# Group-norm statistics of images 2 to 4 gathered in the first image's steps, with a new table of step offsets

## The chip, the cores and the metric

The kernel runs on one core of a Trainium2 chip. The metric is the device time of one execution in microseconds, the median of several runs. Engines are named as the profile names them: PE (TensorE matmul), PEld (its weight loads), DVE (VectorE), ACT (ScalarE), POOL (GpSimd), SP (SyncE, which issues most DMAs).

## What is computed

```python
# x: (4, 64, 64, 96); a group norm per image, then two layers
x = x + conv(gn(x))                    # layer 0
t = tokens(x)                          # (4, 4096, 96)
t = t + attn(ln(t))                    # linear attention, 6 heads
t = t + ffn(ln(t))                     # 96 -> 384 -> 96, values rounded to fp8 and fp16
...
def gn(v, G=32, eps=1e-5):             # mean and variance of each image and group of 3 channels
    m = mean(g, axis=(1, 2, 4)); s = var(g, axis=(1, 2, 4))
    return (g - m) / sqrt(s + eps)
...
def conv(x):                           # a layer norm, a projection, a scan over the 4096 positions
    A, B, C = proj of xn, each (L, 96, 16)
    h = d * (A * h) + d * (B * u)      # one step of the scan
    y = gate * sum(C * h, over 16 states)
```

The group norm needs all 4096 positions of an image before the image's first chunk can begin.

## The kernel before

An image is cut into 8 chunks of 512 positions, so there are 32 chunks, numbered 0 to 31; image b has chunks 8b to 8b+7. A chunk is worked on in 12 steps (`NT`), one for each pair of a state group `sh` (4) and a channel group `cg` (3). Step k belongs to chunk k // 12; its place in the chunk is called r0 to r11. There are 384 steps (`K`).

The core of a step is a pipeline over tiles of 128 x 512. For tile k: PE makes `b_proj`, `a_proj` and `c_proj`, each of three matmuls (L269, into PSUM banks of the tags B, A, and C or D in turn); ACT copies B to SBUF (`b_copy`, L833); POOL multiplies it with the repeated row (`b_mul`, L836, tile `bu`); DVE multiplies A (`a_mul`, L845), scans (`scan`, L852) and multiplies by C (`c_mul`, L876). For the places in `ON_POOL` the last product is split between ACT (`c_copy`, L882) and POOL (`c_mul_pool`, L885). In step s the program emits `b_proj` and `b_copy` of tile s+3, `a_proj` of s+1, `c_proj` of s, `keep` of s-1 (ACT, L862), `b_mul` of s+2, `c_mul_pool` of s-1, `scan` of s, `a_mul` of s+1, `c_mul` of s; after these the step's other calls in the order in which they were entered (`at`), and last `c_copy`. Every engine keeps its order. PSUM has two A banks, one each of B, C and D, and three of the tag M for everything else.

All other work of a chunk is put into steps by hand. The table `AT` gives each piece an offset; a piece of chunk n runs at step 12n plus its offset. Ahead of the chunk (`front`): `load_x`, `centre` and `scale` (POOL, L692 and L695), `stats` (DVE), `rstd` (POOL), `apply` (ACT, L399), `transpose` (PE), `affine` and `upper` (ACT, L710 and L714), `low` (DVE, L719), then the projections d and u with `d_out` (ACT, L731) and `du_out` (DVE, L735). Their rows go to DRAM (`write`, L769) and come back repeated over 128 partitions (`read`, four DMAs at L776, tile `rep`), which `b_mul` and `a_mul` of the chunk need. Behind the chunk (`tail`): `state_sum` (PE, L900), `gated` (DVE), `project_out` (PE, L943), `residual` (DVE, L948), a layer norm, `transpose_a`, `keep`, `spill`, and the Gram matrix. One image later (`ffn`): `fetch`, `attention`, a layer norm, three pairs of `hidden` and `relu`, `project_f`, `round_out`, `bias_out`, `total`, `store`. `gather` adds the partial products of a chunk by DMA (POOL's queue). What does not fit ahead of step 384 is ordered by a planner (`Plan`) that searches 1500 random orders with estimated costs.

The group norm of image 0 is made in a planned start. That of a later image is made during the image before: for each of its 8 chunks, `load_gx` brings the positions into the tile `gx` (one buffer, 192 KB, SP, L130), `sums` transposes them (PE, four transposes, L546) into an M bank, and `sums_out` one step later has ACT sum them and their squares (L577: two passes, each with a read of the accumulator). `first` makes a further transpose of the first chunk for a shift two steps ahead. After the last sum a chain of eleven small pieces, one per step (DVE, POOL, PE, ACT), ends in the tile `gmr` with mean and factor, which `centre` and `scale` use. The sums' places:

```python
when = [s0 + AT["sums"] + NT * n for n in range(NCH)]
if b == 1:
    when = [8, 15, 22, 29, 36, 43, 50, 57]
...
at(max(when[n] - 7, when[n - 1]), load_gx, b, n)
```

With `sums` at -31 these are steps 65, 77, ..., 149 for image 2 and 161, ..., 245 for image 3.

Of the kernel before, what the change touches and what calls it, by code (L numbers as in the profile page):

```python
# [9 lines left out]
F32 = mybir.dt.float32  # L10
# [7 lines left out]
P = 128  # L18
B, H, W, C = 4, 64, 64, 96
# [3 lines left out]
J = 4  # L23
TC = P * J
NCH = L // TC
# [3 lines left out]
NT = NCG * NSH  # L29
# [8 lines left out]


AT = {  # L40

    "load_x": -39, "centre": -25, "scale": -24, "stats": -22, "rstd": -22, "apply": -21,
    "transpose": -14, "affine": -13, "upper": -13, "low": -12, "proj_d": -9, "d_out": -9,
    "proj_u": -9, "du_out": -9, "write": -9, "read": -6, "proj_gate": -3, "gate_out": -1,

    "gather1": 7, "gather2": 11, "gather3": 14,

    "state_sum": 18, "gated": 18, "project_out": 19, "residual": 19, "stats_a": 20,
    "rstd_a": 21, "apply_a": 22, "transpose_a": 33, "keep": 34, "spill": 39, "gram": 24,
    "gram_out": 24, "gram_add": 26,  # L50

    "fetch": 21, "attention": 26, "residual_f": 26, "stats_f": 26, "rstd_f": 27, "apply_f": 29,
    "transpose_f": 30, "quant_in": 31, "hidden0": 37, "relu0": 37, "hidden1": 31, "relu1": 33,
    "hidden2": 38, "relu2": 38, "project_f": 40, "round_out": 40, "bias_out": 40, "total": 46,
    "store": 51,

    "sums": -31, "sums_out": -30,
}
ON_POOL = (0, 2, 7, 8)
XBUFS = 15  # L60


@with_exitstack
def conv_attn_hybrid_kernel(
# [26 lines left out]
    small = ctx.enter_context(tc.tile_pool(name="small", bufs=4))  # L91
# [4 lines left out]
    BUFS = {  # L96
        "x": XBUFS, "gx": 1, "z": 2, "xat": 1,
        "lo": 1, "xs": 2, "xl": 2, "dd": 1, "rep": 2, "gate": 2,
# [112 lines left out]
    for r in range(2):  # L211
        t = const.tile([P, J, CA], F32, tag=f"xa{r}", name=f"xa{r}")
        nc.gpsimd.memset(t[:, :, C:CA], 1.0)
        xa_t.append(t)
        t = const.tile([CA, J, P], F32, tag=f"xal{r}", name=f"xal{r}")
# [3 lines left out]
        t = const.tile([P, J, P], F8, tag=f"xn8{r}", name=f"xn8{r}")  # L219
# [144 lines left out]
    class LayerNorm:  # L364
# [3 lines left out]
            self.eps, self.nm, self.r = eps, nm, None  # L368

        def stats(self, src):  # L370
            st = small.tile([P, J, 6], F32, tag="st", name=f"st_{self.nm}")
            self.mv = small.tile([P, J, 2], F32, tag="mv", name=f"mv_{self.nm}")
            for j in range(J):
                nc.vector.bn_stats(st[:, j, :], src[:, j, :])
            for j in range(J):
                nc.vector.bn_aggr(self.mv[:, j, :], st[:, j, :])
# [153 lines left out]
    def at(step, fn, *args):  # L530
        steps.setdefault(step, []).append((fn, args))
# [4 lines left out]
    class GroupNorm:  # L536
# [104 lines left out]

        def spread_out(self, k0=0, k1=2):
            if k0 == 0:
                t = self.t = small.tile([P, 2, C], F32, tag="gmr", name=f"gmr_{self.b}", bufs=2)
                gn[self.b] = [t[:, k, :].unsqueeze(1).to_broadcast([P, J, C]) for k in range(2)]
            nc.scalar.copy(self.t[:, k0:k1, :], self.spread_ps)

    def group_norm(b, s0):
        q = {}

        def make():
            q["g"] = GroupNorm(b)
            q["g"].first()

        def call(name, *args):
            getattr(q["g"], name)(*args)

        when = [s0 + AT["sums"] + NT * n for n in range(NCH)]  # L660
        if b == 1:
            when = [8, 15, 22, 29, 36, 43, 50, 57]
        if b > 1:
            at(when[0] - 7, load_gx, b, 0)
        at(when[0] - 2, make)
        for n in range(NCH):
            if n:
                at(max(when[n] - 7, when[n - 1]), load_gx, b, n)
            at(when[n], call, "sums", n)
            at(when[n] + AT["sums_out"] - AT["sums"], call, "sums_out", n)  # L670
        chain = (
            ("moments",), ("variances",), ("group_sums", "m"), ("mean",), ("squares",),
            ("group_sums", "v"), ("offset",), ("root",), ("diagonal",), ("spread",), ("spread_out",),
        )
        for n, args in enumerate(chain):
            at(when[-1] + AT["sums_out"] - AT["sums"] + 1 + n, call, *args)


    split, rep, gate = {}, {}, {}

# [103 lines left out]
    def front(b, i, s0, f=None):  # L784
        if f is None:
            f = Front(b, i)
            plan = [
                ("centre", f.centre, nc.gpsimd), ("scale", f.scale, nc.gpsimd), ("stats", f.stats),
                ("rstd", f.ln.rstd), ("apply", f.apply), ("transpose", f.transpose),
                ("affine", f.affine), ("upper", f.upper), ("low", f.low), ("proj_d", f.proj, 2),  # L790
                ("d_out", f.d_out), ("proj_u", f.proj, 0), ("du_out", f.du_out),
                ("write", f.write), ("read", f.read),
            ]
            if (b, i) not in xt:
                plan.insert(0, ("load_x", load_x, b, i))
        else:
            plan = []
        plan += [("proj_gate", f.proj, 1), ("gate_out", f.gate_out)]

        late = {"centre": 0, "scale": 0, "stats": 1, "rstd": 2, "apply": 3}  # L800
        for name, fn, *args in plan:
            step = s0 + AT[name]
            at(max(step, START + late[name]) if name in late else step, fn, *args)
# [4 lines left out]
    class Tile:  # L808


        def __init__(self, k):
# [5 lines left out]
            self.cols = slice(self.sh * P, (self.sh + 1) * P)  # L817
            self.on_pool = self.r in ON_POOL and self.k >= START

# [73 lines left out]
    def state_sum(g, last=None, first=None):  # L893
# [5 lines left out]
        for cg in range(NCG):  # L899
# [10 lines left out]
    end = Plan(  # L910
        {"A": 2, "B": 1, "C": 1, "M": 3, "yg": 1, "xal": 2, "xat": 1, "xn8": 2, "bu": 5, "h": 3, "rep": 2,
         "xs": 2, "xl": 2, "z": 2, "mv": 4},
        {"ACT": 0.5, "DVE": 2.5, "POOL": 1.5},
    )
    end.last = {}
    end.tries = 1500

    def place(plan, s0):

# [474 lines left out]

    for n, fn in enumerate((weights_attention, weights_ffn1, weights_ffn2, weights_bias)):
        at(NT + 8 + NT * n, turned, NT + 8 + NT * n, fn)
    for b in range(B):
        for i in range(NCH):
            g = b * NCH + i
            s0 = g * NT  # L1400
            if g:
                front(b, i, s0, second if g == 1 else None)
            for sh in range(1, NSH):
                if g < N - 1 or sh == 1:
                    at(s0 + AT[f"gather{sh}"], gather, g, sh)
            at(s0 + NT, tail, b, i)
            s = s0 + NCH * NT
            first = min(24, AT["fetch"])
            at(s + first if b == B - 1 else min(s + first, K - 4), ffn, b, i, s)
        if b + 1 < B:  # L1410
            group_norm(b + 1, b * NCH * NT)
        s = (b + 1) * NCH * NT
        at(s if s == K else s + AT["gram_add"] - NT + 1, attn_matrix, b, s)

    def call(step):

        todo = steps.get(step, [])
        n = 0
        while n < len(todo):
            fn, args = todo[n]  # L1420
            fn(*args)
            n += 1
# [73 lines left out]
```

## Time and profile before

| | us |
|---|---|
| runs | 1180.49, 1182.05, 1182.14; median 1182.05 |
| span of the profiled execution, first to last instruction | 1179.2 |
| so outside the span, if its run was like the three | 1.3 to 2.9 |
| scan of step 0 begins, step 383 ends | 34.8, 1104.3 |

| engine | busy us | share of the span |
|---|---|---|
| PE | 1138.6 | 97% |
| PEld | 874.2 | 74% |
| DVE | 1113.3 | 94% |
| POOL | 1040.1 | 88% |
| ACT | 812.9 | 69% |

Busy time of PE includes the modelled ends of matmuls that overlap; the distance from one start to the next tells what PE can do. A group of instructions in the profile has its line, engine, operation and tiles, then the count, the busy time, the mean ns of one, the idle time ahead of it and what ended that. In a timeline each row has start, length, engine, line, operation, tiles and count, and in brackets the idle time ahead and its releaser. Some durations that matter:

| piece | line, engine | mean ns |
|---|---|---|
| `scan` | L852 DVE | 1268 |
| `a_mul`, `c_mul` | L845, L876 DVE | 733, 740 |
| `b_mul`, `c_mul_pool` | L836, L885 POOL | 1343, 1347 |
| `b_copy`, `c_copy` | L833, L882 ACT | 684, 686 |
| sums and squares, with two accumulator reads | L577 ACT | 650 + 193 + 574 + 190 |
| one transpose of `gx` | L546 PE | 272 |
| `apply`, one of four | L399 ACT | 457 |

DMAs (median us from issue to landing): `rep` 7.5 for each of four of 384 KB, `ddd` (the `write`) 3.2, `gx` 7.2, `x` 2.9, a `gather` of 768 KB 6.7.

### The profile page before, as it was taken

The page shows a single profiled execution, that of the slowest core. Times are in us where ns is not written, and L with a number is a line of the kernel's source. Part 1 is how long each engine was busy: PE and PEld are TensorE (multiplying, and loading weights), DVE is VectorE, ACT ScalarE, POOL GpSimd, SP SyncE. Part 2 cuts the span into 40 slices and gives each one's busy share as a digit, 9 for nine tenths or more (in the row PEclk, how much of TensorE's full clock was granted, in tenths as well). Part 3 has the DMA queues.
Part 4 walks back from the last instruction along what each step waited for, and adds up shares of the span by engine and source line. Part 5 has one row for each costly group of instructions (what it writes and reads, how often), then busy time and mean ns, then how long its engine had stood idle before and what let it go on. Part 6 is the DMA issues. An engine that isn't in the chain of part 4 may idle for free. (4 is left out here: it accounts for less than half of the span.)

```text
span 1179.2 us, 19184 instructions
## 1 busy us (share of the span) xinstructions
PE 1138.6 (97%) x5882; PEld 874.2 (74%) x5882; DVE 1113.3 (94%) x2079; ACT 812.9 (69%) x1833; POOL 1040.1 (88%) x1187
## 2 busy tenths in 40 slices
PE   6999999999999999999999999999999999999885
PEld 5777776777777777777777777777777777777563
DVE  6999999999999999999999999999999999999865
ACT  4666655655556777777777778777777777776475
POOL 5798888888889999999999999999999999988575
PEclk8999999999999999999999999999999999999987
DMA  7676776778876777778766776776777768766221
GB/s 184 141 165 145 169 153 156 161 163 178 177 161 148 154 162 166 163 164 191 162 160 151 170 174 159 173 165 156 156 159 159 174 155 182 159 134 146 67 65 51
DMA packets 104288, 182.12 MB, mean 154 GB/s; under 512 B 42637, under 2 KB 50769, under 8 KB 104186
## 3 DMA queue, kind: packets, MB, share of 16 engines
q1 hardware_dynamic: 90060, 106.96, 37.6%
q0 software_dynamic: 13536, 73.93, 31.4%
q8 instruction: 46, 0.75, 0.3%
q14 instruction: 56, 0.46, 0.1%
q10 hardware_dynamic: 590, 0.02, 0.0%
HBM read 69.12 MB, written 24.77 MB: 80 GB/s over the span
## 5 line engine op out<-in xcount | busy, mean ns | idle before, releaser
L836 POOL TENSOR_TENSOR bu<-bu,rep 128x512 f32<-128x512 f32 x384 | 511.9, 1343 | 42.7 <-ACT state L862 32.8
L852 DVE TENSOR_TENSOR_SCAN h<-Aps,state,bu 128x512 f32<-128x512 f32 x336 | 425.9, 1268 | 0.3 <-issue 0.2
L833 ACT ACTIVATE bu<-Bps,b_bac 128x512 f32<-128x512 f32 x384 | 262.8, 684 | 198.8 <-PE Bps L269 193.1
L845 DVE SCALAR_TENSOR_TENSOR Aps<-Aps,b_bac,rep 128x512 f32<-128x512 f32 x384 | 281.6, 733 | 4.7 <-PE Aps L269 4.3
L269 PE MATMUL Bps<-xs,w 128*128 128x512 f32 x768 | 267.1, 429 | 3.8 <-ACT bu L833 3.1
L269 PE MATMUL Aps<-xs,w 128*128 128x512 f32 x768 | 241.8, 396 | 1.2 <-DVE h L852 1.0
L885 POOL TENSOR_TENSOR ch<-ch,h 128x512 f32<-128x512 f32 x126 | 169.8, 1347 | 7.0 <-ACT ch L882 3.3
L269 PEld LDWEIGHTS Aps<-xs,w 128*128 128x128 f32 x768 | 143.9, 188 | 36.9 <-DVE h L852 2.7
L269 PEld LDWEIGHTS Bps<-xs,w 128*128 128x128 f32 x768 | 126.6, 190 | 45.8 <-ACT gx_ps L577 12.6
L269 PE MATMUL Aps<-xl,w 128*128 128x512 f32 x384 | 151.8, 395 | 0.0
L269 PE MATMUL Bps<-xl,w 128*128 128x512 f32 x384 | 151.5, 395 | 0.0
L269 PE MATMUL Dps<-xs,w 128*128 128x512 f32 x384 | 120.7, 395 | 0.0
L269 PE MATMUL Cps<-xs,w 128*128 128x512 f32 x384 | 120.6, 395 | 0.0
L876 DVE SCALAR_TENSOR_TENSOR ch<-Dps,b_bac,h 128x512 f32<-128x512 f32 x160 | 118.6, 741 | 0.4
L891 POOL DMA_DIRECT2D ch<-ch x94 | 88.9, 946 | 1.4 <-DMA ch<-ch 1.1
L269 PEld LDWEIGHTS Bps<-xl,w 128*128 128x128 f32 x384 | 72.3, 188 | 17.5
L269 PEld LDWEIGHTS Aps<-xl,w 128*128 128x128 f32 x384 | 72.1, 188 | 17.6
L269 PEld LDWEIGHTS Dps<-xs,w 128*128 128x128 f32 x384 | 72.1, 188 | 17.5
L269 PEld LDWEIGHTS Cps<-xs,w 128*128 128x128 f32 x384 | 72.1, 188 | 17.5
L882 ACT ACTIVATE ch<-Cps,b_bac 128x512 f32<-128x512 f32 x94 | 64.5, 686 | 24.2 <-PE Cps L269 24.2
L269 PE MATMUL Cps<-xl,w 128*128 128x512 f32 x192 | 75.8, 395 | 0.0
L269 PE MATMUL Dps<-xl,w 128*128 128x512 f32 x192 | 75.6, 394 | 0.0
(200 smaller groups left out, 2049.4 us busy)
## 6 DMA issues: line engine op xcount, KB each, us to landing
ch<-ch POOLq DMA_DIRECT2D x94, 768.0 KB, 6.7
rep<-ddd SPq DMA_DIRECT2D x124, 384.0 KB, 7.5
ddd<-dd SPq DMA_DIRECT2D x31, 384.0 KB, 3.2
xl<-lo SPq DMA_DIRECT2D x62, 128.0 KB, 2.4
x<-in_x_dram SPq DMA_DIRECT2D x32, 192.0 KB, 2.9
xatd<-xat SPq DMA_DIRECT2D x32, 192.0 KB, 3.6
xal<-xatd SPq DMA_DIRECT2D x32, 192.0 KB, 5.4
out_dram<-o SPq DMA_DIRECT2D x32, 192.0 KB, 2.5
```

The lines of the kernel that those rows point to most:

```text
L269: nc.tensor.matmul(ps, lhsT=wt[:, n], rhs=mv, start=(n == 0), stop=(n == 2))
L833: nc.scalar.activation(self.bu, self.b_ps, AF.Identity, bias=self.bias(0))
L836: nc.gpsimd.tensor_tensor(self.bu, self.bu, rep[self.b, self.i][:, 1, self.cg], ALU.mult)
L845: nc.vector.scalar_tensor_tensor(self.a_ps, self.a_ps, self.bias(1), rep[self.b, self.i][:, 0, self.cg], ALU.add, ALU.mult,)
L852: nc.vector.tensor_tensor_scan(self.h, self.a_ps, self.bu, 0.0 if self.i == 0 else state[self.sh, self.cg], ALU.mult, ALU.add,)
L876: nc.vector.scalar_tensor_tensor(self.slot(), self.c_ps, self.bias(2), self.h, ALU.add, ALU.mult)
L882: nc.scalar.activation(self.ch, self.c_ps, AF.Identity, bias=self.bias(2))
L885: nc.gpsimd.tensor_tensor(self.ch, self.ch, self.h, ALU.mult)
L891: nc.gpsimd.dma_start(chs[g, 0], chs.pop((g, sh)), accum_op=ALU.add)
```

## The change

The sums of images 1, 2 and 3 get places of their own in a table `GN_AT`: images 1 and 2 by turns in steps 8 to 59, image 3 in steps 64 to 114. One function `group_norms` orders all 24 by step; each load is entered four steps ahead of its sum, but not ahead of the step of the sum before it, since `gx` still has one buffer. `gmr` has three buffers in place of two, and the layer norms' `st` two in place of four. The chain of each image follows its own last sum. The offsets of `AT` are new, among them `apply`, `du_out`, `write`, `gate_out`, the three `gather`s, `transpose_a`, `spill`, `fetch`, `hidden0`, `relu1` and `store`, and `ON_POOL` has place 4 in place of 2. The number of the planner's tries gets a name and keeps its value.

```diff
@@ -38,26 +38,26 @@
 AT = {
-    "load_x": -39, "centre": -25, "scale": -24, "stats": -22, "rstd": -22, "apply": -21,
+    "load_x": -40, "centre": -25, "scale": -24, "stats": -22, "rstd": -22, "apply": -18,
     "transpose": -14, "affine": -13, "upper": -13, "low": -12, "proj_d": -9, "d_out": -9,
-    "proj_u": -9, "du_out": -9, "write": -9, "read": -6, "proj_gate": -3, "gate_out": -1,
-    "gather1": 7, "gather2": 11, "gather3": 14,
-    "state_sum": 18, "gated": 18, "project_out": 19, "residual": 19, "stats_a": 20,
-    "rstd_a": 21, "apply_a": 22, "transpose_a": 33, "keep": 34, "spill": 39, "gram": 24,
-    "gram_out": 24, "gram_add": 26,
-    "fetch": 21, "attention": 26, "residual_f": 26, "stats_f": 26, "rstd_f": 27, "apply_f": 29,
-    "transpose_f": 30, "quant_in": 31, "hidden0": 37, "relu0": 37, "hidden1": 31, "relu1": 33,
-    "hidden2": 38, "relu2": 38, "project_f": 40, "round_out": 40, "bias_out": 40, "total": 46,
-    "store": 51,
-    "sums": -31, "sums_out": -30,
+    "proj_u": -9, "du_out": -7, "write": -6, "read": -6, "proj_gate": -3, "gate_out": -3,
+    "gather1": 6, "gather2": 10, "gather3": 13, "state_sum": 18, "gated": 18, "project_out": 19,
+    "residual": 19, "stats_a": 20, "rstd_a": 21, "apply_a": 22, "transpose_a": 35, "keep": 35,
+    "spill": 36, "gram": 24, "gram_out": 25, "gram_add": 25, "fetch": 18, "attention": 26,
+    "residual_f": 26, "stats_f": 26, "rstd_f": 27, "apply_f": 29, "transpose_f": 30,
+    "quant_in": 30, "hidden0": 34, "relu0": 37, "hidden1": 31, "relu1": 32, "hidden2": 38,
+    "relu2": 38, "project_f": 40, "round_out": 41, "bias_out": 41, "total": 44, "store": 49,
+    "sums": -35, "sums_out": -33,
 }
-ON_POOL = (0, 2, 7, 8)
+GN_AT = {
+    1: [8, 15, 22, 28, 36, 43, 50, 57],
+    2: [12, 19, 25, 32, 39, 46, 53, 59],
+    3: [64, 69, 79, 84, 92, 102, 107, 114],
+}
+GX_AHEAD = 4
+ON_POOL = (0, 4, 7, 8)
 XBUFS = 15
+END_TRIES = 1500
 @with_exitstack
@@ -368,7 +368,7 @@
             self.eps, self.nm, self.r = eps, nm, None
         def stats(self, src):
-            st = small.tile([P, J, 6], F32, tag="st", name=f"st_{self.nm}")
+            st = small.tile([P, J, 6], F32, tag="st", name=f"st_{self.nm}", bufs=2)
             self.mv = small.tile([P, J, 2], F32, tag="mv", name=f"mv_{self.nm}")
             for j in range(J):
                 nc.vector.bn_stats(st[:, j, :], src[:, j, :])
@@ -641,40 +641,36 @@
         def spread_out(self, k0=0, k1=2):
             if k0 == 0:
-                t = self.t = small.tile([P, 2, C], F32, tag="gmr", name=f"gmr_{self.b}", bufs=2)
+                t = self.t = small.tile([P, 2, C], F32, tag="gmr", name=f"gmr_{self.b}", bufs=3)
                 gn[self.b] = [t[:, k, :].unsqueeze(1).to_broadcast([P, J, C]) for k in range(2)]
             nc.scalar.copy(self.t[:, k0:k1, :], self.spread_ps)
-    def group_norm(b, s0):
+    def group_norms(place):
         q = {}
-        def make():
-            q["g"] = GroupNorm(b)
-            q["g"].first()
-        def call(name, *args):
-            getattr(q["g"], name)(*args)
-        when = [s0 + AT["sums"] + NT * n for n in range(NCH)]
-        if b == 1:
-            when = [8, 15, 22, 29, 36, 43, 50, 57]
-        if b > 1:
-            at(when[0] - 7, load_gx, b, 0)
-        at(when[0] - 2, make)
-        for n in range(NCH):
-            if n:
-                at(max(when[n] - 7, when[n - 1]), load_gx, b, n)
-            at(when[n], call, "sums", n)
-            at(when[n] + AT["sums_out"] - AT["sums"], call, "sums_out", n)
+        def make(b):
+            q[b] = GroupNorm(b)
+            q[b].first()
+        def call(b, name, *args):
+            getattr(q[b], name)(*args)
         chain = (
             ("moments",), ("variances",), ("group_sums", "m"), ("mean",), ("squares",),
             ("group_sums", "v"), ("offset",), ("root",), ("diagonal",), ("spread",), ("spread_out",),
         )
-        for n, args in enumerate(chain):
-            at(when[-1] + AT["sums_out"] - AT["sums"] + 1 + n, call, *args)
+        order = sorted((s, b, n) for b, steps_of in place.items() for n, s in enumerate(steps_of))
+        for k, (s, b, n) in enumerate(order):
+            if k:
+                at(max(s - GX_AHEAD, order[k - 1][0]), load_gx, b, n)
+            if n == 0:
+                at(s - 2, make, b)
+            at(s, call, b, "sums", n)
+            at(s + 1, call, b, "sums_out", n)
+            if n == NCH - 1:
+                for c, args in enumerate(chain):
+                    at(s + 2 + c, call, b, *args)
     split, rep, gate = {}, {}, {}
@@ -913,7 +909,7 @@
         {"ACT": 0.5, "DVE": 2.5, "POOL": 1.5},
     )
     end.last = {}
-    end.tries = 1500
+    end.tries = END_TRIES
     def place(plan, s0):
@@ -1394,6 +1390,7 @@
     for n, fn in enumerate((weights_attention, weights_ffn1, weights_ffn2, weights_bias)):
         at(NT + 8 + NT * n, turned, NT + 8 + NT * n, fn)
+    group_norms(GN_AT)
     for b in range(B):
         for i in range(NCH):
             g = b * NCH + i
@@ -1407,8 +1404,6 @@
             s = s0 + NCH * NT
             first = min(24, AT["fetch"])
             at(s + first if b == B - 1 else min(s + first, K - 4), ffn, b, i, s)
-        if b + 1 < B:
-            group_norm(b + 1, b * NCH * NT)
         s = (b + 1) * NCH * NT
         at(s if s == K else s + AT["gram_add"] - NT + 1, attn_matrix, b, s)
```

## The prediction

> **What bounds the kernel now.** I read the windows by chunk first, then DVE's waits, then the timeline of one step. A chunk is 12 steps, `r0` to `r11`; chunk n starts at step 12n, and an entry of `AT` with offset o runs at step 12·chunk + o. The windows are chunks 4, 6, 19 and 27 (columns: window, length, then busy us of PE, PEld, DVE, ACT, POOL):
>
> ```profile
> 165.60:201.10 35.50, 32.93 (x158) 24.86 (x157) 32.80 (x59) 20.11 (x50) 30.00 (x32) 1.00 0.76 167
> 234.40:266.10 31.70, 31.68 (x153) 24.46 (x152) 31.48 (x53) 18.85 (x46) 28.07 (x31) 1.00 0.74 164
> 669.05:702.98 33.93, 33.93 (x179) 26.19 (x179) 32.98 (x62) 26.55 (x61) 31.91 (x37) 1.00 0.74 168
> 939.40:972.90 33.50, 33.50 (x175) 25.82 (x175) 32.97 (x63) 25.09 (x57) 31.89 (x37) 1.00 0.74 163
> ```
>
> PE and DVE are both full. Chunk 19 has one group-norm sum (L546 on PE, L577 on ACT), chunk 27 none: DVE works 32.98 and 32.97 us, the same, yet the chunk is 0.43 us shorter. So DVE isn't the limit there. Where it waits:
>
> ```profile
> DVE x L948 <- PE o_ps L943: 8.4, 10, 1.0
> ...
> DVE x L948 <- PE o_ps L943: 5.2, 9, 0.9
> ```
>
> (first 410 to 740 us, with group-norm sums in most chunks; then 740 to 1060, without). Step r7 of chunk 27 shows why:
>
> ```profile
> 958.60 0.74 PE L269 MATMUL Bps<-xs,w 128*128 128x512 f32 x2
> 959.18 0.39 PE L269 MATMUL Bps<-xl,w 128*128 128x512 f32 x1
> 959.41 0.63 PE L269 MATMUL Aps<-xs,w 128*128 128x512 f32 x2
> 959.88 0.40 PE L269 MATMUL Aps<-xl,w 128*128 128x512 f32 x1
> 960.11 0.63 PE L269 MATMUL Dps<-xs,w 128*128 128x512 f32 x2
> 960.58 0.39 PE L269 MATMUL Dps<-xl,w 128*128 128x512 f32 x1
> 960.92 0.38 PE L1124 MATMUL h_ps<-xq,w_q 96*128 96x512 fp8e5 x1
> 961.13 1.03 PE L943 MATMUL o_ps<-w_o,yg 97*128 97x96 f32 x8
> 962.20 0.56 DVE L948 TENSOR_TENSOR x<-o_ps,x 128x384 f32<-128x384 f32 x1 [0.49 <-PE o_ps L943]
> ```
>
> PE's starts follow each other by 0.23 us with no hole: DVE waits 0.49 us because PE, working through its list without a stop, reaches `project_out` late. **PE is the bound**, DVE right behind it (0.5 us per chunk with the FFN, 0.2 in image 0). The other losses are single stalls of PE. In chunk 4 ACT has `d_out`, `apply` and a group-norm sum in one step:
>
> ```profile
> 175.05 0.69 ACT L731 ACTIVATE dd<-dug_ps,b_dug 96x512 f32<-96x512 f32 x1 [1.26 <-PE dug_ps L269]
> 175.64 1.53 ACT L399 ACTIVATE z<-z,nmr_c,rstd_c 128x96 f32<-128x96 f32 x4
> ...
> 178.45 0.67 ACT L833 ACTIVATE bu<-Bps,b_bac 128x512 f32<-128x512 f32 x1
> ...
> 179.18 0.73 PE L269 MATMUL Bps<-xs,w 128*128 128x512 f32 x2 [1.38 <-ACT bu L833]
> ```
>
> `b_copy` (L833) is late, the one B bank stays taken, PE stands 1.38 us.
>
> **What the skill says.** The Trainium skill, "Perfetto Trace Analysis", Identifying the Most-Contended Engine, holds matmul busy time for a bad measure and LDWEIGHTS busy for a good one. Here the latter is 26 of 33.5 us (77%) and would hide the bound; the starts decide. The same page (Tensor Engine Instruction) calls ACT, DVE and GpSimd strict FIFO, which the ACT lines agree with. "DMA: Bandwidth & Descriptors", Two DMAs through the same engine are not ordered, has the issuing engine wait on the first DMA's semaphore before it issues a dependent one; here SP stands 54.3 us in 30 waits, about 1.8 each, between `write` and `read`, with all of SP's later DMAs behind.
>
> **The sums, moved.** 24 sums remain 24. One costs PE 0.35 us (four transposes, 59.18 to the next start at 59.53) and 0.09 for the restart: 0.44, the 0.43 of the windows. Before, chunk 0 has one, 1 to 4 have 2, 1, 2, 2, chunks 5 to 20 one each. After: chunks 0 to 9 have 1, 4, 3, 4, 4, 2, 1, 2, 2, 1. Eleven sums leave chunks 10 to 20: 11 × 0.43 = −4.7 us. The same eleven enter chunks 1 to 8, where PE is full with one sum (31.68 of 31.70): +4.7, less at most 0.2 of slack in about five chunks, −1. So **−1 in place of −4.7**. The ACT part, 0.65 + 0.19 + 0.57 + 0.19 = 1.6 us, finds room on average (ACT idles 12.8 us in chunk 6), not in every step.
>
> **Stalls that go.** In chunk 4 DVE waits 0.66 and 0.58 us behind the pile-up above, 0.34 and 1.03 after the sum at step 57: 2.6. Around step 161 the chain of image 2 meets the first sum of image 3: about 0.9. Together **−3.5**.
>
> **Stalls that come.** `gx` has one buffer; each load waits for the transposes of the sum before.
>
> ```profile
> L130 SPq DMA_DIRECT2D gx<-in_x_dram x24: 352/373/1147, 37.9 to 701.7; - x24
> ...
> DMA to landing us min/median/max: 4.8/7.2/11.4
> ```
>
> Before, the next use is 7 to 12 steps off. Now the steps alternate between images 1 and 2, three or four apart, and in three places two: load at 8 for `first` at 10, 57 for 59, 60 for 62. PE goes from its end of step 8 to that of step 10 in 5.3 us (59.18 to 64.50); the load issued at 59.80 took 7.2. Stall 7.8 − 5.3 = 2.5, of which some replaces a hole of 0.87 there now: 2. At 57 a `rep` read is again under way: 1.7. At 60 none is, and the same bytes for `x` take 2.8 (median): 0. Steps 19→22 and 43→46 give PE 8.0 and 9.0 us, but SP holds the load behind the `write`/`read` pair, now at r6: 1 each. The other gaps, 6.5 us and up: 0.5 in all. Sum **+6.2**; from 0 (all land in 2.8) to +17 (all in 11.4).
> ACT doubles up again: sums_out at 54 meets `apply`, at 58 and 70 `apply_a`, at 47 `affine`, `upper` and `keep`: 3.1 to 3.5 us in a step against 3.8 at step 51 before, which cost 1.2. Half of it, 4 × 0.6 = **+2.4** (0 to 5). Queued behind is `b_copy`, PE waits for that, DVE for PE.
>
> **The table.** `du_out` goes from r3 to r5, two steps or 5.0 us later, and the `rep` read with it (SP issues when the write has landed, not when the step comes). Now, in chunk 27, `du_out` ends at 951.79, the read goes out from 955.14 to 956.5 and takes 4.1/7.8/9.5 us; the first `b_mul` that needs it starts at 968.40, the first `a_mul` at 971.58. Landed by 966.0 at the worst; 5.0 later is 971.0: POOL waits up to 2.6 us, 0.9 at the median, DVE 0. POOL is idle 1.6 per chunk, and each `bu` is finished over 1.4 us ahead of its scan; the tightest, at r6, gains 1.3 because its neighbour's `c_mul_pool` moves from r3 to r5 (tile r2 to r4). I take 0, covered by that lead; from −1 to +25 (0.8 per chunk if it is gone). `relu1` at r8 ahead of `c_copy` makes `b_copy` end when PE wants B at r10: 0 to +3, taken as +0.5. `apply` at r6 fits ACT's hole of 2.76 us there. `gather` a step earlier, `fetch`, `store`, `total`: SP and POOL work that PE doesn't wait for, covered by a step's slack: 0. `st` in two buffers is written and read by DVE alone, `gmr` in three: 0. No job changes side of step 384, so the drain after the last scan, some 75 us, stays: 0 ± 1.
>
> **Sum.** −1 − 3.5 + 6.2 + 2.4 + 0.5 = +4.6 on the span of 1179.2, 1183.8. The runs lie 1.3 to 2.9 above that span, the median 2.9: 1186.7.
>
> **Rivals.** (1) Faster: the loads land quickly. Where `gx` takes the 2.8 us of `x` the +6.2 is gone, and if ACT's steps stay as harmless as step 23 is now (0.69 + 0.73 + 0.58 + 1.6 = 3.6 us of ACT, no wait of DVE), the +2.4 too: −4; the new order may also close PE's 0.1 us restarts by pairing small products, some −3. 1182 − 7 = 1175. For it: few landings are recorded. Against: the one at step 8 took 7.2. It decides at a landing of about 5.3 us. (2) Slower by much: the late `rep` read. If landings grow by 0.7 us over 9.5, a scan or `a_mul` waits 0.5 in each of 31 chunks, +15: 1200. Against: it needs all to be at the upper end. (3) The stalls cancel, or the moves do nothing to PE's list: 1182.
>
> **Numbers.** About 0.2%, 2.4 us, is what a measurement tells from no change. Main case 0.48 (1181 to 1191, a fifth of it inside 0.2%), rival 1 0.27, rival 2 0.20, rival 3 0.05. Faster 0.27; same 0.15; slower 0.58. The main case's own range is 1181 to 1191; with the others, 1175 to 1200.
>
> **What would show it.** Right: chunks 10 to 20 at 33.5 us, DVE's `x` wait at 0.5 there; chunks 1 to 4 at 33 us or more with PE without holes except at L546, waiting for `gx` (steps 10 and 59), and at B after L577. Wrong: a PE hole in every chunk of images 2 to 4 or POOL waiting over 2.6 us at L836 (rival 2), or image 1 no longer than now (rival 1).

## The result and the profile after

The changed kernel takes 1256.07 us (median of 4 runs, 1255.35 to 1260.94), the kernel before 1182.1 beside it: ratio 1.063, 95% interval 1.061 to 1.066. It is slower by 74 us; the forecast was 1186.7, with 1200 as its upper end. The profiled execution spans 1254.9 us (before: 1179.2). The title counts the images from 1, the text from 0; and the sums of image 3 end at step 114, so they run on into the steps of image 1, which begin at 96. Lines of the changed kernel stand four lower than those of the kernel before: `b_mul` is L832 (L836), `a_mul` L841 (L845).

The windows of chunks 4, 6, 19 and 27 after the change (columns as in the prediction: window, length, then busy us of PE, PEld, DVE, ACT, POOL, then clock, DMA share, GB/s):

```profile
184.52:222.47 37.95, 36.45 (x183) 28.10 (x182) 36.70 (x59) 25.34 (x64) 27.52 (x29) 1.00 0.70 147
258.95:294.37 35.42, 33.43 (x161) 25.14 (x160) 31.62 (x53) 20.43 (x50) 28.42 (x31) 1.00 0.74 155
723.27:759.47 36.20, 35.11 (x186) 26.81 (x185) 33.09 (x63) 26.46 (x60) 31.53 (x37) 1.00 0.69 151
1006.44:1042.03 35.59, 34.08 (x175) 25.42 (x174) 33.09 (x63) 25.11 (x58) 31.84 (x37) 1.00 0.68 154
```

Chunk 27 has no sum, before or after, and the same work (PE 175 matmul rows, DVE 63 rows and 33.09 us for 32.97). It grew from 33.50 to 35.59 us. So the loss isn't the sums' work, and it is not confined to the chunks that got them. DVE, which had half a microsecond of idle time in such a chunk, now has 2.5. What ended it, in DVE's waits of images 2 and 3 (436 to 794 us):

```profile
DVE Aps L841 <- DMA rep<-ddd: 11.1, 5, 2.8
DVE Aps L841 <- PE Cps L269: 4.0, 1, 4.0
DVE Aps L841 <- PE Bps L269: 2.9, 1, 2.9
```

and in the last part (794 to 1113 us):

```profile
DVE Aps L841 <- DMA rep<-ddd: 8.1, 4, 2.9
DVE Aps L841 <- issue: 4.2, 2, 2.3
...
DVE x L944 <- PE o_ps L939: 0.8, 2, 0.4
```

The old wait for `o_ps`, the mark of PE as the bound, is nearly gone; in its place `a_mul` waits for `rep`. Some of these waits have other names, since the program's view names the event that came last. The timeline of chunk 27 shows it: of its rows, these are SP's, POOL's gather, the last scan ahead of the stall with the two instructions that end it, and a wait of PE.

```profile
1024.08 0.32 SPq L765 DMA_DIRECT2D ddd<-dd  x1
1027.54 1.79 SPq L772 DMA_DIRECT2D rep<-ddd  x4
1029.37 1.48 SPq L1089 DMA_DIRECT2D xal<-xatd  x1
...
1027.66 0.88 POOL L887 DMA_DIRECT2D ch<-ch  x1
...
1037.07 1.27 DVE L848 TENSOR_TENSOR_SCAN h<-Aps,state,bu 128x512 f32<-128x512 f32 x1
...
1039.96 0.73 PE L269 MATMUL Bps<-xs,w 128*128 128x512 f32 x2 [1.05 <-ACT bu L829]
...
1040.67 0.76 DVE L841 SCALAR_TENSOR_TENSOR Aps<-Aps,b_bac,rep 128x512 f32<-128x512 f32 x1 [2.33 <-issue]
1040.70 1.29 POOL L832 TENSOR_TENSOR bu<-bu,rep 128x512 f32<-128x512 f32 x1 [2.94 <-ACT xnt_ps L706]
```

The last `rep` landed at 1040.49. POOL and DVE, which have no work in common there, start together 0.2 us later: they had both stood for that landing, 2.9 and 2.3 us. The row says `issue` and `xnt_ps`; the landing beside it says what it was. The read went out at 1027.54 and gather1 of the chunk ahead at 1027.66, in the same step. In the kernel before, 4.6 us lay between them (reads from 955.14, gather at 959.79). The view of the read gives who waited for it and its time to landing (min/median/max), first in the kernel before, where the list of those who waited is empty, then after. The landings are those of 14 or 15 of the 124 reads; for the others the trace doesn't tell one:

```profile
who waited for it (us, times):
...
DMA to landing us min/median/max: 3.7/7.5/9.5
```

```profile
  POOL bu L832: 63.1, 16
  DVE Aps L841: 32.8, 16
...
DMA to landing us min/median/max: 7.7/10.4/12.3
```

What a shared DMA looks like can be read by taking the DMA view of two short stretches of chunk 27. The read alone, 1029.5 to 1031.5 us (columns: queue, packets, MB, share of the 16 engines):

```profile
q1 hardware_dynamic: 267, 0.51, 98.7%
q0 software_dynamic: 1, 0.01, 1.5%
```

and with the gather, 1032.2 to 1035.4 us:

```profile
DMA packets 183, 0.73 MB, mean 228 GB/s; under 512 B 9, under 2 KB 9, under 8 KB 183
...
q0 software_dynamic: 91, 0.56, 87.1%
q1 hardware_dynamic: 92, 0.17, 21.8%
```

Over this stretch, 91 packets of POOL's queue went beside 92 of SP's, near one for one. But 0.56 MB against 0.17: the gather's packets are 6144 bytes, the read's 2048. Together they move 228 GB/s, about what the read moves alone, and the read falls from 255 to 53. The Trainium skill, "DMA: Bandwidth & Descriptors", Queues, rings and completion order, says that each engine takes turns between queues packet by packet. The stretch as a whole fits that; half microseconds of it don't show a steady one for one (8 packets of POOL's against 30 of SP's from 1032.0, 13 against 8 from 1033.0, 12 against 15 from 1034.5). The prediction didn't use that sentence, and should have. For when the read ends, the shares matter less than the bytes. An estimate: the read alone holds 217 GB/s over 4.5 us (the same view of the kernel before, 958.0 to 962.5 us), and gather1's 768 KB at that rate are 3.6 us, put in ahead of the read's end. The median landing grew by 2.9, less than that, perhaps because a part of the four reads is through by then.

The kernel before has the same meeting, at the end of the read only. There gather1's packets begin 7.9 us after the read goes out (4.0 in the change), and from 963.0 to 966.0 us, where the last part of the read lands, the view has

```profile
q0 software_dynamic: 100, 0.61, 99.8%
q1 hardware_dynamic: 53, 0.07, 12.9%
```

So the 9.5 us, the longest landing of the kernel before, was itself that of a read beside gather1. Where the gather keeps out of the read (experiments 5 and 8 below), the longest is 8.6 and 8.5.

### The profile page after: what moved, and what is told of

It is laid out like the page before. It is cut to its first block, busy times and chain, and to the rows that moved or that the text cites. A ratio compares the mean times of both kernels' runs of the same rounds, so it can differ in the third digit from the quotient of the medians.

```text
span 1254.9 us, 19280 instructions
## 1 busy us (share of the span) xinstructions
PE 1160.9 (93%) x5882; PEld 878.8 (70%) x5882; DVE 1121.1 (89%) x2079; ACT 820.0 (65%) x1833; POOL 1039.6 (83%) x1187
## 5 line engine op out<-in xcount | busy, mean ns | idle before, releaser
L832 POOL TENSOR_TENSOR bu<-bu,rep 128x512 f32<-128x512 f32 x384 | 541.1, 1436 | 124.1 <-DMA rep<-ddd 63.1
L829 ACT ACTIVATE bu<-Bps,b_bac 128x512 f32<-128x512 f32 x384 | 263.0, 685 | 195.7 <-PE Bps L269 172.6
L841 DVE SCALAR_TENSOR_TENSOR Aps<-Aps,b_bac,rep 128x512 f32<-128x512 f32 x384 | 282.2, 735 | 76.2 <-DMA rep<-ddd 32.8
L269 PE MATMUL Aps<-xs,w 128*128 128x512 f32 x768 | 248.2, 404 | 15.8 <-DVE h L848 14.9
L269 PEld LDWEIGHTS Aps<-xs,w 128*128 128x128 f32 x768 | 140.8, 189 | 67.6 <-DVE h L848 37.8
L881 POOL TENSOR_TENSOR ch<-ch,h 128x512 f32<-128x512 f32 x126 | 178.0, 1413 | 6.0 <-ACT ch L878 3.9
L878 ACT ACTIVATE ch<-Cps,b_bac 128x512 f32<-128x512 f32 x94 | 64.2, 683 | 35.8 <-PE Cps L269 35.5
L399 ACT ACTIVATE xa<-x,nmr_a,rstd_a 128x96 f32<-128x96 f32 x124 | 47.8, 457 | 53.7 <-POOL nmr_a L387 53.6
## 6 DMA issues: line engine op xcount, KB each, us to landing
rep<-ddd SPq DMA_DIRECT2D x124, 384.0 KB, 10.4
```

The lines of the kernel that those rows point to most:

```text
L269: nc.tensor.matmul(ps, lhsT=wt[:, n], rhs=mv, start=(n == 0), stop=(n == 2))
L399: nc.scalar.activation(dst[:, j, 0:C], src[:, j, :], AF.Identity, bias=self.nmr[:, j : j + 1], scale=self.r[:, j : j + 1], **kw,)
L829: nc.scalar.activation(self.bu, self.b_ps, AF.Identity, bias=self.bias(0))
L832: nc.gpsimd.tensor_tensor(self.bu, self.bu, rep[self.b, self.i][:, 1, self.cg], ALU.mult)
L841: nc.vector.scalar_tensor_tensor(self.a_ps, self.a_ps, self.bias(1), rep[self.b, self.i][:, 0, self.cg], ALU.add, ALU.mult,)
L878: nc.scalar.activation(self.ch, self.c_ps, AF.Identity, bias=self.bias(2))
```

## The experiments

All ran beside the kernel before (1181.4 to 1182.4 us in the three groups). Landings are those of `rep`, min/median/max, of 14 or 15 reads each.

**1. du_out and write put back.**

```diff
-    "du_out": -7, "write": -6,
+    "du_out": -9, "write": -9,
```

> The changed kernel with du_out and write back at -9 (the rest of the new table and the new places of the sums stay). Theory A (in every chunk the `rep` read goes out 5 us later, runs into gather1's transfer, lands at 10 us instead of 7.5, and POOL's b_mul and DVE's a_mul wait for it, 1.5 to 2 us in some 28 chunks, about 50 us): the waits of L832 and L841 for rep go, 1200 to 1212 us. Theory B (the new places of the sums carry the loss) and theory C (other entries of the table: relu1, apply, the transposes, ON_POOL): within 5 us of 1256.

1183.87 us, ratio 1.002 (1.001 to 1.003); landings 3.9/7.9/9.1. Some 72 of the 74 us are gone with these two entries, although the sums stay in their new places; theory A had given 44 to 56. From chunk 11 to 29 all take 33.6 to 33.9 us, but for the first two of images 2 and 3. Theories B and C fall as causes of the loss. The waits for `gx` fall with it, a link that I hadn't seen. In the changed kernel and in this one, waits of PE:

```profile
PE gx_ps L546 <- DMA gx<-in_x_dram: 16.2, 5, 5.7
```

```profile
PE gx_ps L546 <- DMA gx<-in_x_dram: 0.8, 1, 0.8
```

**2. The same two entries alone, put into the kernel before.**

```diff
-    "du_out": -9, "write": -9,
+    "du_out": -7, "write": -6,
```

> The kernel before with du_out at -7 and write at -6 alone; gather1 stays at 7. Theory A with the collision at any of the two places of gather1: the read now runs from 962 to 968 on the clock of chunk 27, gather1's packets at 963 to 967, so they still meet: 1222 to 1240 us. Theory A where the earlier gather is needed as well: the read lands 5 us later, at 971, and POOL waits about 0.9 us per chunk, mostly absorbed: 1182 to 1195. Theories B and C: 1182 within 3.

1273.48 us, 1.078 (1.075 to 1.080); landings up to 12.7. The direction is theory A's, the size beyond what it gave: +92, not +40 to +58. The two entries are enough by themselves, with gather1 at either place. Two waits of this run stand in the list neither of the kernel before nor of the change, DVE's for `c_mul_pool` and PE's for `xl`:

```profile
DVE h L852 <- POOL ch L885: 20.1, 21, 1.7
PE dug_ps L269 <- DMA xl<-lo: 16.4, 24, 1.8
```

**3. The gathers put back.**

```diff
-    "gather1": 6, "gather2": 10, "gather3": 13,
+    "gather1": 7, "gather2": 11, "gather3": 14,
```

> The changed kernel with gather1, gather2, gather3 back at 7, 11, 14 (du_out and write stay late). If the read is late because gather1, one step earlier, takes the DMA engines ahead of it: the read has 2.5 us more alone, lands 2 to 4 us earlier, and most of the wait goes: 1205 to 1230 us. If the read is late only because du_out is late, or the fetch is what it collides with: 1250 to 1258. Theories B and C: 1256 within 5.

1242.83 us, 1.053 (1.049 to 1.057): 13 us better, less than expected, and landings much as in the change, 4.6/10.3/12.1. In chunk 27 the gather's packets begin 6.6 us after the read goes out (4.0 in the change), and all 128 of them still fall ahead of its landing. Not everywhere: in chunks 21 and 23 they begin 7.9 and 8.3 us after it, only 33 fall in, the read's last part takes 8.0 and 7.9 us, and these chunks take 33.1 and 33.5 us, while 20, 22 and 24 take 35.0, 35.8 and 36.8. Chunks without the loss and chunks with it stand side by side in one run: what counts is whether the gather gets into the read.

**4. Only the new places of the sums.**

```diff
+GN_AT = {1: [8, 15, ...], 2: [12, 19, ...], 3: [64, 69, ...]}
...
-            group_norm(b + 1, b * NCH * NT)
+    group_norms(GN_AT)
```

> The kernel before with the new places of the group norm sums (GN_AT, GX_AHEAD, the three gmr and two st buffers), all other entries of the table as before. Theory B: PE waits for gx, whose one buffer can't be loaded ahead, in image 0 (steps 10, 22, 46, 59 and others), and the sums leave images 1 and 2: 1182 + 17 to 20 in chunks 0 to 9, minus 11 x 0.43 later: 1193 to 1202 us. The forecast's own step (+6.2 for gx, -3.5 for stalls that go, -1, +2.4): 1186. If the loss sits in the table alone: 1182 or less.

1185.49 us, 1.0036 (1.0027 to 1.0046): +4.1 us, where theory B had 11 or more and the forecast's terms for this part come to +4.1. Chunks 10 to 20 take 33.3 to 33.5 us except chunk 17 (chunk 19 was 33.93), as forecast.

**5. The gathers moved out of the read's way.**

```diff
-    "gather1": 6, "gather2": 10, "gather3": 13,
+    "gather1": 9, "gather2": 12, "gather3": 15,
```

> The changed kernel with the gathers moved out of the read's way: gather1, gather2, gather3 at 9, 12, 15 (6, 10, 13 in the change). du_out and write stay late. Theory A1 (it is the sharing: gather1's 768 KB take the DMA engines in the middle of the read, which then ends 4 us later): the read runs alone, `rep` lands at 19 instead of 24 us after the step r3 begins, before the first b_mul that needs it, and nearly all of the loss goes: 1184 to 1200 us. Theory A2 (du_out two steps late is enough by itself, shared or not): 1240 to 1256.

1208.41 us, 1.022 (1.020 to 1.024). Landings 4.0/7.7/8.6: with the read as late as in the change, the landing is back to that of before, and DVE has no wait for `rep` in the list. 48 us return. Not all, and 8 us short of theory A1's range: the collision has moved. PE's waits in this run:

```profile
PE y_ps L896 <- DMA ch<-ch: 7.5, 9, 1.4
PE Bps L269 <- ACT bu L829: 7.1, 23, 0.7
PE dug_ps L269 <- DMA xl<-lo: 5.8, 10, 1.6
```

The gathers now reach the state sum late, and they take the engines from `xl` (128 KB each), whose median rose from 3.8 to 6.2 us. So this run can't separate cleanly; experiment 8 does.

**6. du_out early, write late.**

```diff
-    "du_out": -7, "write": -6,
+    "du_out": -9, "write": -6,
```

> The changed kernel with du_out alone back at -9; write stays at -6. If what counts is when the data is ready (SP has nothing else in its queue between -9 and -6 that would hold it, so it sends the write as soon as du_out ends): as with both back, 1181 to 1190 us. If the place of the write in the table holds it (theory: the step number delays SP): 1240 to 1256.

1186.07 us, 1.004 (1.002 to 1.005), landings 4.1/7.8/9.3. `du_out` is the entry that costs. SP waits for data, not for steps, so the write's own offset counts for about 2 us.

**7. One step late.**

```diff
-    "du_out": -7, "write": -6,
+    "du_out": -8, "write": -8,
```

> The changed kernel with du_out and write at -8: one step later than before, one and a half earlier than in the change; gathers stay at 6, 10, 13. Theory A1: the read's packets start 2.5 us earlier than in the change, most of them are through when gather1 starts, rep lands at about 20.5 us after r3, and the first b_mul that needs it starts at 23.7: no wait, 1184 to 1192 us. If the loss grows in proportion to the lateness (29 us per step of 2.5 us): 1213 to 1220.

1189.54 us, 1.005 (1.003 to 1.007). Landings 4.1/8.2/11.2: the gather already lengthens some, POOL waits for `rep` 17.8 us in 11 times, and DVE never appears in that list. So the loss has an edge: 6 us against experiment 1 for the first step, 67 for what follows. Since DVE has no wait for `rep` here, POOL's lead takes up the first.

**8. No gather1.** The transfer of gather1 is left out, so a quarter of the states is missing from the sum.

```diff
-        nc.gpsimd.dma_start(chs[g, 0], chs.pop((g, sh)), accum_op=ALU.add)
+        t = chs.pop((g, sh))
+        if sh > 1:
+            nc.gpsimd.dma_start(chs[g, 0], t, accum_op=ALU.add)
```

> The changed kernel, du_out and write late, without the transfer of gather1 (its 768 KB per chunk are not added to the state sum; gather2 and gather3 stay at 10 and 13). Theory A1 (the read loses its bandwidth to gather1): the read runs alone and lands at 19 to 20 us after r3 as with the gathers late, without the new waits that those made at the state sum and at `xl`: 1182 to 1190 us. Theory A2 (the lateness alone): 1230 or more.

1179.21 us, 0.9965 (0.995 to 0.998), landings 3.8/7.8/8.5: du_out and write as late as in the change, and no loss. That is 77 us off by leaving out one transfer, of which some 5 are beyond experiment 1, where most of gather1's packets come after the read; they may be gather1's own work, which isn't shown. POOL is also freed of 32 issues of some 1 us, but experiment 5 keeps them and has the landing back too. POOL still waits for the late `rep`:

```profile
POOL bu L832 <- ACT state L858: 20.1, 20, 2.4
POOL bu L832 <- DMA rep<-ddd: 20.0, 19, 2.7
```

at most 2.7 us, and DVE doesn't. Lateness alone is covered by POOL's lead; lateness and the gather together are not.

**9. The kernel before, read late, with the new ON_POOL.**

```diff
-ON_POOL = (0, 2, 7, 8)
+ON_POOL = (0, 4, 7, 8)
```

(on top of experiment 2)

> The kernel before with du_out at -7, write at -6 (1273 us by itself) and ON_POOL (0, 4, 7, 8) in place of (0, 2, 7, 8). The forecast gave the move of c_mul_pool from tile r2 to r4 credit for 1.3 us of POOL's lead per chunk. If that is what makes the late read dearer in the kernel before (+92) than in the changed kernel (+72): 1273 falls to 1245 to 1255. If it is the fetch at 21 or another entry: 1270 or more.

1263.00 us, 1.067 (1.065 to 1.070): 10.5 us of relief, half of what was expected. So `ON_POOL` is part of what makes experiment 2 dearer than the change, and not all. The traces say more than the times: DVE's wait for `c_mul_pool`, 20.1 us in experiment 2, is gone here, and PE's for `xl` stays, 14.8 us in 22 times. Which other entry of the table spares the change that wait was not tested.

**10. Two gx buffers with the new places of the sums.**

```diff
-        "x": XBUFS, "gx": 1, ...
+        "x": XBUFS, "gx": 2, ...
```

(on top of experiment 4)

> The kernel before with the new places of the sums and two gx buffers in place of one. The forecast's term for gx was +6.2 of the +4.1 measured for the new places; the waits of PE for gx in the trace of that run are 2.6, 1.5 and 1.1 us. If the waits for gx are what the new places cost: 1179 to 1182 us. If it is ACT's and DVE's work in image 0: 1185, no change.

1182.42 us, 0.9994 (0.998 to 1.0005): 3.1 us less than with one. But the kernel before was 1.0 us slower beside this run than beside experiment 4; against it the loss went from 4.1 to nothing, and in the two traces image 0 takes 5.1 us less. So with the read on time the waits for `gx` cost 3 to 5 us.

**11. The sums of image 1 away from ACT's full steps.**

```diff
-            when = [8, 15, 22, 29, 36, 43, 50, 57]
+            when = [8, 15, 22, 29, 36, 43, 49, 56]
```

> The kernel before with the last two sums of image 1 one step earlier (49 and 56 in place of 50 and 57), so that their ACT part no longer falls into the step of `apply` (51) and of `apply_a` (58). If the pile-up on ACT makes the stalls of chunk 4 (0.66, 0.58, 0.34 and 1.03 us of DVE): 1179 us, 2.6 below. If they come from d_out and apply alone: 1181.4, no change.

1180.58 us, 0.9989 (0.9981 to 0.9997): 1.2 us better, half of what was expected. DVE's idle time in chunk 4 fell from 2.70 to 0.37 us, but the chunk only from 35.53 to 34.55. The rest went into one instruction of DVE, L585 of the chain, that takes 1.82 us here in place of 0.17: time that the view counts as busy (the last section has such a row). It is the fastest complete version that was run, by a little.

**12. Meant to be the fastest:** the new table with du_out and write at -9, the old code of the sums, 49 and 56.

> A version meant to be the fastest: the new table with du_out and write back at -9, the old places of the sums with the last two of image 1 at 49 and 56. By adding up: 1180.6 for the sums apart, minus 1.6 (the new table without du_out and write, 1183.9 against 1185.5): 1179.0 us. If the new table gains only where the new sums stand: 1180.6 to 1182.

1189.88 us, 1.006 (1.004 to 1.008): 8 to 9 us worse than experiment 11, not better. Chunk 5 takes 38.0 us (33.1 there), with 2.6 us of DVE behind `d_out` and 2.0 behind PE. The effects of table and places don't add up.

## Why the prediction was wrong

The scans' time by image (from its first scan to that of the next, for image 3 to the end of the last scan, in us) shows where each part lies:

| kernel | image 0 | 1 | 2 | 3 |
|---|---|---|---|---|
| before | 263.0 | 268.7 | 271.7 | 266.0 |
| only the new sums (4) | 274.0 | 266.3 | 268.5 | 266.0 |
| the change, read on time (1) | 269.3 | 267.8 | 269.2 | 266.3 |
| the change | 293.9 | 283.9 | 285.1 | 278.8 |

**The step that failed is "The table", in its words "Landed by 966.0 at the worst; 5.0 later is 971.0" and "I take 0, covered by that lead".** The prediction moved the read on the clock and kept its duration. It did follow SP's queue, but it counted each `gather` as "SP and POOL work that PE doesn't wait for, covered by a step's slack: 0": as an issue on POOL, and not as 768 KB on the same 16 engines. Moving the read by 5 us put it into gather1; landings went from 3.7/7.5/9.5 to 7.7/10.4/12.3. The "worst" of 9.5 was no bound: it was measured beside the end of a gather. The term was 0, with +25 as its worst; it measured some +72 (experiment 1), and leaving out gather1 alone takes it away (experiment 8). The bound itself, "POOL waits up to 2.6 us ... DVE 0", held to 0.1 us where the read kept its duration (experiment 8: 2.7, DVE none). So the reasoning about POOL's lead was right, and the assumption under it wrong.

**Rival 2** had the mechanism and its sign ("If landings grow by 0.7 us over 9.5"), at a chance of 0.20 and 0.5 us per chunk. What it said against itself, "it needs all to be at the upper end", was the error: it took that for unlikely, but a collision that recurs in chunk after chunk moves all of them up; the shortest recorded landing went from 3.7 to 7.7. 72 us over 31 chunks are 2.3 each. Of the two marks that the prediction named for it, POOL's came (up to 6.6 us at L832):

```profile
POOL bu L832 <- DMA rep<-ddd: 63.1, 16, 6.6
```

PE's is seen in chunk 27 (1.05 us, behind `b_copy`); the list has 17 such waits in the whole run, so a hole in every chunk isn't shown.

**The sums.** The forecast's four terms, -1, -3.5, +6.2 and +2.4, come to +4.1, and the part alone measured +4.1 (3.2 to 5.4). That is luck, since the terms themselves were not so good. `gx` measured 3 to 5 for 6.2 (experiment 10), so the other three were between +1 and -1 together, not -2.1. "Stalls that go" is the one that can be seen to fail: DVE's 2.6 us of idle time in chunk 4 did not go, it is 2.5 with the new places (experiment 4). Chunks 10 to 20 fell to 33.5 as forecast.

**gx in the changed kernel.** At step 10, ahead of `first`, PE waited 2.5 us (forecast 2). The sums at 22, 46, 59, 84 and 107 waited 4.7, 5.7, 1.3, 1.6 and 2.9, together the 16.2 of the row shown; the first three were named, with 1, 1 and 1.7. With the read on time (experiment 1) step 10 keeps its 2.5, 22 has 0.8, and the others have nothing to show. So most of it came with the late read. `load_gx` stands in SP's queue behind the write and the read; which part is SP's queue and which the shared engines wasn't taken apart.

**The rest of the table.** Experiments 1 and 4 differ by all other entries: -1.6 us, hardly beyond the noise of the two, where +0.5 was taken. It is made of 4.7 us less in image 0 and about 0.15 more in most later chunks. The drain stayed at 75 us in experiment 1.

**PE as the bound** was right for the kernel before, and it is a statement about the order of that kernel only. Its weak side was to treat 0.5 us of DVE's slack as if the next limit were DVE's own work; the next limit was a DMA.

## What to carry to other kernels

When a transfer is moved in time, write down which other transfers are in flight in its new place, on all queues and with their bytes, and lengthen its landing by their bytes over the rate that the trace shows: here 768 KB over 217 GB/s, 3.6 us, where the median grew by 2.9. A landing time from a profile holds only for the neighbours that it was measured with. And a lead that covers a delay is used up whole before anything shows, so a loss measured for one step of delay (here 6 us) says nothing of what follows (67).

## What the runs showed of the hardware

- Two queues that shared the DMA engines came out near packet for packet, not byte for byte: in 3.2 us of chunk 27, 91 packets of 6144 bytes against 92, nearly all of 2048. The queue with the small packets kept 0.17 of 0.73 MB, a quarter. This is one stretch; no run changes the size of the packets.
- A small DVE instruction was recorded as lasting until POOL's work beside it ended. In the changed kernel:

```profile
218.34 4.22 DVE L585 TENSOR_SCALAR gt<-gt 96x2 f32<-96x2 f32 x1
218.77 1.56 POOL L832 TENSOR_TENSOR bu<-bu,rep 128x512 f32<-128x512 f32 x1
220.02 1.26 POOL L688 TENSOR_TENSOR z<-x,gmr 128x384 f32<-128x384 f32 x1
220.99 1.53 POOL L832 TENSOR_TENSOR bu<-bu,rep 128x512 f32<-128x512 f32 x1
```

It takes 0.17 to 0.30 us in the kernel before and 4.22 here, and ends when the third POOL instruction in a row does. The Trainium skill, "SBUF — State Buffer", SBUF: two separate sides, describes a port pair that DVE, in some modes, and GpSimd lock against each other for a whole instruction. The rows fit that, and show the wait inside DVE's busy time, over three instructions. The row of 1.82 us in experiment 11 (195.41 to 197.23) ends like this too: POOL's L692 beside it ends at 197.19. No run here tests the cause. In the changed kernel the instruction comes three times, once for each image from 1 on, and takes 6.6 us of DVE's busy time in all, for 0.8 before.
